# Projecting two bands at once and taking a group mean out earlier, in a four-layer convolution kernel

## The chip, the cores and the metric

The kernel runs as one launch on one core of a Trainium2 chip, in fp32 throughout. The metric is the device time of that launch in microseconds (us). The kernel before takes 4968.51 us, the median of three runs (4963.12 to 4970.23); the profiled execution that is read below spans 4964.9 us. The core has five engines with their own instruction queues: TensorE (PE in the profile, with its weight loads as PEld), VectorE (DVE), ScalarE (ACT), GpSimd (POOL) and SyncE (SP, which here only issues transfers).

## The reference

The input is 4 images of 384 channels and 64x64 positions. Four residual layers follow one another, each `x = x + layer(group_norm(x))` with 32 groups of 12 channels. Two of them matter here.

Layer 1 projects the normalised image to 384 hidden channels, filters every 8x8 patch of them in the frequency domain, runs a depthwise 3x3 convolution, multiplies one half of the channels (through a gelu) with the other half, and projects the 192 products back:

```
t = einsum('bchw,oc->bohw', x, w_in)
...                                     # patch filter, depthwise 3x3
x1, x2 = t[:, :hid // 2], t[:, hid // 2:]
g = gelu(x1) * x2
return einsum('bchw,oc->bohw', g, w_out)    # 192 -> 384 channels
```

Layer 3 is a depthwise 7x7 convolution whose 49 taps differ for every image and channel: `gamma * (x_w * w_mix * Nx) + beta`, where `x_w` comes from the mean and the maximum of each channel. Because `beta` is the same for all 49 taps, the kernel computes it as a 7x7 box sum, and the rest as a convolution with the fixed taps `w_mix` that is scaled per image and channel afterwards.

Layer 0 is a convolution with an attention over the 4096 positions; layer 2 consists of depthwise 3x3 and 5x5 convolutions and two channel projections (384 to 768 and back). Their code is not changed.

## The kernel before

The code is a Python builder that writes instructions in a program order; a list scheduler then orders them on each engine, by priority (the order of writing, unless a block is under `tc.high_priority()`), by what each waits for and by its estimate of when an engine is free. The engines then work through their queues in order. Tiles come from pools: a tag with `bufs=2` has two buffers in turn, and a new tile of the tag waits until the last reader of the tile before the previous one is done.

There are four stages, one after the other:

- `phase_a` (0 to 2533 us): layers 0 and 1. `side_by_side` (L529) takes the 64 steps of the attention of image b, and between them pieces of `others`: the norm of image b+1, its q, k and v, and layer 1 of image b-1. Each piece yields a cost in us of TensorE time, and `per_step` spreads the sum of these costs over the 64 steps. A step of the attention is four score products over 32 rows each (L715, under high priority), exponentials on ScalarE (L723) and four products over 128 rows (L752). Layer 1 of the last image runs alone, from 2290 us on.
- `phase_b` (to 3191 us): the depthwise convolutions of layer 2.
- `phase_ef` (to 4195 us): its channel projections, dense TensorE work.
- `phase_g` (to the end): the end of layer 2, the group norm and layer 3.

**Layer 1's projection back.** `layer1` (L797) works through 8 bands of 8 image rows. `band_taps` (L926) leaves the gated products of a band in two tiles: 128 channels in `acc[1]`, and 64 channels in rows 64 to 127 of `acc[2]`. `band_out` (L959), one piece per band, adds the projection to the band of x: for each of the three output blocks of 128 channels, a product over 128 rows (L965) and one over 64 rows (L966) accumulate in one PSUM tile, and VectorE adds it to x (L969). The PSUM tag "m" of this stage has two buffers. Each block yields 2.0 us.

**The beginning of phase_g.** `x2_of` (L1671) makes the input of layer 3 from what phase_ef left in memory, for one image and one block of 128 channels at a time, in four quarters of 1024 positions. ScalarE scales the second projection's result into PSUM (L1688, two of 512), VectorE adds it to x (L1691), ScalarE sums the squares (L1693) and VectorE takes the maximum (L1694). The finished tile of 2 MB goes to memory (L1696). The first block (j = 0) is brought into "strips", the layout of the convolution, by `to_strips` (L1699), one image behind: ScalarE subtracts the group's mean into another tile (L1710), TensorE transposes it in blocks of 128 (L1720), and ScalarE (L1727) and VectorE (L1725) copy the results to `z`.

**The rest of phase_g.** `conv7` (L1730) convolves 8 channels at a time: it loads their taps (`wmix`, L1735), expands them to matrices (L1744, every third on GpSimd) and multiplies (L1757). 48 such calls follow one another, 16 for each block of channels. In between, the first 16 take pieces of `x2_of` for the other two blocks; the other 32 take pieces of `boxes` (L1772), the box sums. `half_strips` (L1633) reads x2 of the next block from memory, scales and shifts it on ScalarE (L1649), transposes it and copies it to `z` (L1658, L1660). In `boxes`, x has its mean still in it, so constants of 6 or 7 means (`off`) are subtracted with every sum on VectorE (L1812 to L1823), and the padding is filled with means on ScalarE (L1793). L1837 adds the box sums to x, L1847 adds the convolution's result.

The transfers of x, of the taps and of the strips are all issued by SyncE, in one queue.

Of the kernel before, what the change touches and what calls it, by code (L numbers as in the profile page):

```python
# [27 lines left out]
N = H * W  # L28
# [132 lines left out]
def _layout(i):  # L161
# [38 lines left out]
    w_out_t[64:, 1] = w_out[P:]  # L200
# [26 lines left out]
class _Builder:  # L227
# [301 lines left out]
    def side_by_side(self, b, steps, others):  # L529

        per_step = ((176 if b else 0) + (42 if b + 1 < B else 0)) / 64
        ahead = 0.0
        for n, _ in enumerate(steps):
            while others is not None and ahead < n * per_step:
                piece = next(others, None)
                if piece is None:
                    others = None
                else:
                    ahead += piece
        for _ in others or ():  # L540
            pass
# [255 lines left out]
    def layer1(self, b):  # L797
# [9 lines left out]
        for n in range(-2, 4 * 11):  # L807
# [35 lines left out]
            if w == 0 and h > 2:  # L843
                k = h - 3
                yield from self.band_out(b, acc.pop(k), k, st)
# [80 lines left out]
    def band_taps(self, h, alone, acc):  # L926
# [9 lines left out]
        for j in range(NJ):  # L936
            acc.append(self.wk("acc", "acc", 5))
# [16 lines left out]
            if j == 2:  # L954
                nc.scalar.activation(acc[0][64:P], acc[2][0:64], AF.Gelu)
                nc.vector.tensor_mul(acc[2][64:P], acc[2][64:P], acc[0][64:P])
            yield

    def band_out(self, b, acc, h, st):  # L959

        nc = self.nc
        x = self.block("xa_out", self.xa[b], h, "xo", 2)
        for o in range(NJ):
            m = self.pa("out_m1") if b == B - 1 else self.pm("out_m")
            nc.tensor.matmul(m, lhsT=self.w_out[:, 0, o * P : (o + 1) * P], rhs=acc[1], start=True, stop=False)  # L965
            nc.tensor.matmul(  # L966
                m, lhsT=self.w_out[64:P, 1, o * P : (o + 1) * P], rhs=acc[2][64:P], start=False, stop=True
            )
            nc.vector.tensor_add(x[:, o], x[:, o], m)  # L969
            yield 2.0  # L970
        self.stats(st, x, h)
        nc.gpsimd.dma_start(self.x1[b][:, :, h * 512 : (h + 1) * 512], x)
# [487 lines left out]
    def phase_g(self):  # L1460
# [8 lines left out]
        with ExitStack() as ctx:  # L1469
# [26 lines left out]
            self.s_s, self.s_b = (cp.tile([P, NJ, B], F32, tag=k, name=k) for k in ("s_s", "s_b"))  # L1496
            self.a_pair = cp.tile([P, NJ, 2, 2, 2], F32, tag="a_pair", name="a_pair")

            self.gm = cp.tile([P, NJ, B], F32, tag="gm", name="gm")
            self.off = cp.tile([P, NJ, B, 3], F32, tag="off", name="off")  # L1500
# [7 lines left out]
            behind = iter(())  # L1508
            for b in range(B):
                for x in self.x2_of(0, b):  # L1510
                    next(behind, None)
                for _ in behind:
                    pass
                behind = self.to_strips(0, b, x)
            for _ in behind:
                pass
            self.pair_scales(1)
# [10 lines left out]
            for j in range(NJ):  # L1528
# [12 lines left out]
                if j == 0:  # L1541
# [3 lines left out]
                    self.pair_scales(2)  # L1545
# [5 lines left out]
    def group_means(self):  # L1551
# [4 lines left out]
        for i, k in enumerate((-6.0, -7.0, 2.0)):  # L1556
            nc.vector.tensor_scalar(self.off[:, :, :, i], self.gm, k, None, ALU.mult)
        nc.gpsimd.memset(self.s_s, 1.0)
        nc.vector.tensor_scalar(self.s_b, self.gm, -1.0, None, ALU.mult)
# [12 lines left out]
    def factors(self):  # L1572
# [3 lines left out]
        d, avg, mx = tile_of("g_d"), tile_of("g_avg"), tile_of("g_max")  # L1576
        nc.vector.tensor_sub(avg, self.mean2, self.gm)
# [9 lines left out]
        nc.vector.tensor_sub(mx, mx, self.gm)  # L1587
# [32 lines left out]
        nc.vector.tensor_copy(self.s_s[:, 2], self.a_s[:, 2])  # L1620
        nc.vector.scalar_tensor_tensor(self.s_b[:, 2], self.gm[:, 2], -1.0, self.a_s[:, 2], ALU.mult, ALU.mult)

    def pair_scales(self, j):

        for half in range(2):
            for u in range(2):
                for k, v in enumerate((self.s_s, self.s_b)):
                    self.nc.gpsimd.dma_start(
                        self.a_pair[64 * u : 64 * u + 64, j, k, half],
                        v[64 * half : 64 * half + 64, j, u::2],  # L1630
                    )

    def half_strips(self, j, half):  # L1633

        nc = self.nc
        for pair in range(2):
            for part in range(3):
# [10 lines left out]
                s, b = (self.a_pair[:, j, k, half, pair : pair + 1] for k in range(2))  # L1648
                nc.scalar.activation(y[:, inside], y[:, inside], AF.Identity, bias=b, scale=s)  # L1649
                for i, (k0, n) in enumerate(((0, 4), (4, 4), (8, 3))):  # L1650
# [6 lines left out]
                    if i == 1:  # L1657
                        nc.vector.tensor_copy(zv.rearrange("p c k b -> p k b c"), mv)  # L1658
                    else:
                        nc.scalar.copy(zv, mv.rearrange("p k b c -> p c k b"))  # L1660
# [10 lines left out]
    def x2_of(self, j, b):  # L1671

        nc = self.nc
# [3 lines left out]
        else:  # L1677
            x = self.gx_tile("x2")
            nc.sync.dma_start(x, self.wx[b][:, j])
        for q in range(4):  # L1680
# [4 lines left out]
            for v in range(2):  # L1685
                m = self.pm("x2_m")
                part = slice(q * 1024 + v * 512, q * 1024 + v * 512 + 512)
                nc.scalar.activation(  # L1688
                    m, h[:, v * 512 : v * 512 + 512], AF.Identity, bias=at(self.g0), scale=at(self.gh)
                )  # L1690
                nc.vector.tensor_add(x[:, part], x[:, part], m)  # L1691
# [3 lines left out]
            yield None  # L1695
        nc.gpsimd.dma_start(self.scratch["x2"][b][j], x)  # L1696
        yield x

    def to_strips(self, j, b, x):  # L1699

        nc = self.nc

        for part in range(3):
            y = self.gt_p.tile([P, 11 * P], F32, tag="y", name="ax2", bufs=2)
            lo, hi = (22 * part - 1) * W, (22 * part + 21) * W
            if part == 0:
                nc.gpsimd.memset(y[:, 0:W], 0.0)
            if part == 2:
                nc.gpsimd.memset(y[:, N - lo :], 0.0)
            nc.scalar.activation(  # L1710
                y[:, max(lo, 0) - lo : min(hi, N) - lo],
                x[:, max(lo, 0) : min(hi, N)],
                AF.Identity,
                bias=self.s_b[:, j, b : b + 1],
                scale=self.s_s[:, j, b : b + 1],
            )
            for i, (k0, n) in enumerate(((0, 4), (4, 4), (8, 3))):
                m = self.pm("strip_m")
                for k in range(n):
                    nc.tensor.transpose(m[:, k * P : (k + 1) * P], y[:, (k0 + k) * P : (k0 + k + 1) * P], self.ident)  # L1720
                mv = m.rearrange("p (k c) -> p k c", c=P)[:, 0:n, :]
                at = 1 + 11 * part + k0
                zv = self.z[:, :, at : at + n, b]
                if i == 1:
                    nc.vector.tensor_copy(zv.rearrange("p c k -> p k c"), mv)  # L1725
                else:
                    nc.scalar.copy(zv, mv.rearrange("p k c -> p c k"))  # L1727
            yield

    def conv7(self, j, c0):  # L1730
# [3 lines left out]
        wmix = self.gt_p.tile([P, 8 * 64], F32, tag="wmix", name="wmix")  # L1734
# [151 lines left out]
```

## Time and profile before

| stage | us | PE busy | DVE busy | ACT busy | POOL busy | GB/s |
|---|---|---|---|---|---|---|
| attention with layer 1 (640 to 2290 us) | 1650 | 1599.19 | 916.29 | 761.41 | 60.15 | 57 |
| layer 1 of the last image alone (2290 to 2533) | 243 | 231.16 | 181.61 | 103.06 | 10.19 | 92 |
| x2 and strips of the first block (4204 to 4290) | 86 | 36.52 | 58.40 | 80.84 | 8.74 | 304 |
| first 16 conv7 calls, x2 of two blocks (4290 to 4496) | 206 | 157.24 | 133.73 | 120.86 | 64.29 | 332 |
| next 16 calls with boxes (4496 to 4740) | 244 | 209.35 | 207.55 | 88.53 | 137.83 | 208 |
| last 16 calls with boxes (4740 to 4965) | 225 | 188.27 | 204.85 | 45.70 | 102.47 | 245 |

The table is the busy time of the engines in the stages that the change touches. Busy times of one engine are unions, so that two instructions that overlap count once; a PE busy all the time need not be at its peak, [...]. An fp32 product appears as two MATMUL passes, so 96 products are 192 instructions.

### The profile page before, as it was taken

What the parts mean: (1) busy time and instruction counts of PE and PEld (TensorE: products, weight loads), DVE (VectorE), ACT (ScalarE), POOL (GpSimd) and SP (SyncE); (2) the same over time, 40 slices, a digit from 0 to 9 for tenths busy, and PEclk for the clock granted to TensorE, in tenths of its full rate; (3) what the DMA queues carried; (4) which work ended last, traced back from release to release, by engine and by line L of the source; (5) the groups of instructions that cost most, each with busy time, mean ns of one, the idle gap of its engine ahead of it and who ended that gap; (6) DMA issues with size and microseconds to landing.
All of it is one profiled execution on the core that took longest, in us unless ns stands there. A gap on an engine that the chain in (4) does not pass through costs nothing.

```text
span 4964.9 us, 47732 instructions
## 1 busy us (share of the span) xinstructions
PE 4552.7 (92%) x17665; PEld 2564.5 (52%) x17665; DVE 2769.8 (56%) x4438; ACT 2136.4 (43%) x2873; POOL 777.5 (16%) x593
## 2 busy tenths in 40 slices
PE   5999999999999999998989999699999998677988
PEld 2343444434443344444557888444444443577888
DVE  5322465644666445555867778655531112667898
ACT  4444344454444444444435666411123333764321
POOL 1000000000000000000025555100000001125554
PEclk9999999999999999998989999799999999699999
DMA  5210211211111111112338999776664443896776
GB/s 169 73 47 30 85 54 55 72 56 39 64 64 51 55 45 58 58 57 78 120 122 276 291 292 292 250 278 256 256 245 157 153 152 132 316 343 203 239 255 227
DMA packets 346710, 752.64 MB, mean 152 GB/s; under 512 B 22779, under 2 KB 173158, under 8 KB 337510
## 3 DMA queue, kind: packets, MB, share of 16 engines
q1 hardware_dynamic: 280728, 475.46, 30.1%
q0 software_dynamic: 32640, 151.28, 7.9%
q10 hardware_dynamic: 33102, 122.77, 6.3%
q8 instruction: 143, 2.34, 0.2%
q14 instruction: 97, 0.79, 0.0%
HBM read 447.16 MB, written 302.25 MB: 151 GB/s over the span
## 4 chain that ended last, share of the span: by engine, by line
PE 45%; DVE 9%; DMA 4%; ACT 3%; issue 3%; POOL 1%; SPq 0%; ACTq 0%; DVEq 0%; POOLq 0%
PE h_s L1380 10%; PE h_m L1432 10%; PE conv_m L1156 9%; PE av L752 3%; PE t_m L871 2%; PE conv_m L1757 2%; DVE acc L948 2%; DMA wmix<-in_mix_t 1%; DMA g_h<-h 1%; PE out_m L966 1%; PE proj_m L785 1%; PE sc_s L715 1%; DVE toep L1744 1%; PE taps_m L941 1%; DVE toep L1137 1%
## 5 line engine op out<-in xcount | busy, mean ns | idle before, releaser
L752 PE MATMUL av<-probs,vt 128*128 128x512 f32 x2048 | 965.6, 607 | 0.0
L723 ACT ACTIVATE probs<-sc_s 128x1024 f32<-128x1024 f32 x512 | 500.9, 1021 | 789.8 <-PE av L752 783.7
L752 PEld LDWEIGHTS av<-probs,vt 128*128 128x128 f32 x2048 | 371.7, 192 | 468.1 <-issue 461.0
L1156 PE MATMUL conv_m<-toep,z 128*128 128x256 f32 x2304 | 519.4, 385 | 10.6 <-DVE toep L1137 5.1
L948 DVE SCALAR_TENSOR_TENSOR acc<-band,vecs,acc 128x512 f32<-128x512 f32 x708 | 496.9, 747 | 45.7 <-POOL band L909 39.9
L1432 PE MATMUL h_m<-f_h,cm_w_t 128*128 128x512 f32 x1152 | 496.7, 595 | 8.7 <-ACT f_h L1422 8.7
L1156 PEld LDWEIGHTS conv_m<-toep,z 128*128 128x128 f32 x2304 | 439.4, 193 | 71.0 <-DVE z L1089 4.9
L1757 PE MATMUL conv_m<-toep,z 128*128 128x128 f32 x3072 | 392.8, 286 | 42.1 <-DVE toep L1744 19.2
L1757 PEld LDWEIGHTS conv_m<-toep,z 128*128 128x128 f32 x3072 | 378.7, 202 | 44.4 <-POOL toep L1744 18.2
L1380 PE MATMUL h_s<-e_tok,cm_w_t 128*128 128x512 f32 x768 | 363.4, 596 | 5.5 <-DVE e_tok L1365 5.5
L1137 POOL TENSOR_TENSOR toep<-w,band 128x1536 f32<-128x1536 f32 x94 | 324.0, 3447 | 278.0 <-PE conv_m L1156 232.0
L1432 PEld LDWEIGHTS h_m<-f_h,cm_w_t 128*128 128x128 f32 x1152 | 220.0, 191 | 285.4 <-issue 273.3
L715 PE MATMUL sc_s<-q,k 32*128 32x512 f32 x2048 | 296.3, 647 | 21.9 <-ACT probs L723 21.4
L1440 DVE BATCH_NORM_STATS2 h_st<-f_h 128x6 f32<-128x512 f32 x96 | 66.4, 694 | 429.1 <-ACT f_h L1439 429.1
L871 PE MATMUL t_m<-w_in_t,xb 128*128 128x384 f32 x768 | 276.7, 495 | 3.4 <-DVE coef L888 2.1
L1387 ACT COPY e_h<-h_s 128x1024 f32<-128x1024 f32 x96 | 97.2, 1012 | 401.5 <-PE h_s L1380 401.5
L785 PE MATMUL proj_m<-xm,w_proj_t 128*128 128x512 f32 x576 | 265.2, 599 | 4.6 <-DVE xm L738 3.5
L792 DVE SCALAR_TENSOR_TENSOR x_res<-proj_m,bn_c,x_res 128x512 f32<-128x512 f32 x96 | 71.8, 748 | 319.0 <-PE proj_m L785 315.9
L1380 PEld LDWEIGHTS h_s<-e_tok,cm_w_t 128*128 128x128 f32 x768 | 147.0, 192 | 189.5 <-issue 183.2
L1389 DVE BATCH_NORM_STATS2 h_st<-e_h 128x6 f32<-128x512 f32 x192 | 123.4, 685 | 202.8 <-ACT e_h L1387 202.8
L871 PEld LDWEIGHTS t_m<-w_in_t,xb 128*128 128x128 f32 x768 | 142.9, 192 | 139.0 <-issue 59.3
L1380 PE MATMUL h_s<-z,cm_w_t 128*128 128x512 f32 x384 | 196.2, 593 | 0.0
(380 smaller groups left out, 6206.2 us busy)
## 6 DMA issues: line engine op xcount, KB each, us to landing
d<-d_o ACTq DMA_DIRECT2D x96, 512.0 KB
c_d<-d SPq DMA_DIRECT2D x96, 512.0 KB
hid<-e_h ACTq DMA_DIRECT2D x16, 3072.0 KB
f_h<-hid SPq DMA_DIRECT2D x16, 3072.0 KB
x_in<-in_x SPq DMA_DIRECT2D x96, 256.0 KB
x_res<-in_x SPq DMA_DIRECT2D x32, 768.0 KB
xa<-x_res POOLq DMA_DIRECT2D x32, 768.0 KB, 3.9
xa_in<-xa SPq DMA_DIRECT2D x32, 768.0 KB
```

What stands on the lines that cost most here:

```text
L715: nc.tensor.matmul(s[:, g], lhsT=k4[32 * g : 32 * g + 32, c], rhs=q[i][32 * g : 32 * g + 32], start=True, stop=True,)
L723: nc.scalar.activation(p[:, h * 1024 : (h + 1) * 1024], s[:, 2 * h : 2 * h + 2].rearrange("p a b -> p (a b)"), AF.Exp, scale=0.25,)
L752: nc.tensor.matmul(av, lhsT=vt[:, 4 * c + v, :], rhs=p[:, v * 512 : (v + 1) * 512], start=c == 0 and v == 0, stop=c == 7 and v == 3,)
L785: nc.tensor.matmul(m, lhsT=self.w_proj[:, j, o * P : (o + 1) * P], rhs=xm[:, j], start=j == 0, stop=j == NJ - 1,)
L871: nc.tensor.matmul(m[:, 0:C], lhsT=xb[:, j], rhs=self.w_in[:, j, :], start=j == 0, stop=j == NJ - 1,)
L948: nc.vector.scalar_tensor_tensor(out, src(j, k), w, done, ALU.mult, ALU.add)
L1137: eng.tensor_tensor(t, self.w53[:, at : at + 192].rearrange("p (m n) -> p m n", n=8).unsqueeze(2).to_broadcast([P, 24, 8, 8]), band.rearra ...
L1156: nc.tensor.matmul(m[:, c * 256 : (c + 1) * 256], lhsT=self.z_[:, at : at + P], rhs=t[:, 12 * c + 4 * i : 12 * c + 4 * i + 4].rearrange("p ...
L1380: nc.tensor.matmul(s[:, v, :], lhsT=w1[:, j, o * P : (o + 1) * P], rhs=t[j][:, v * 512 : (v + 1) * 512], start=j == 0, stop=j == NJ - 1,)
L1389: nc.vector.bn_stats(st[:, o, 8 * b + 2 * i + v, :], h[:, o, v * 512 : (v + 1) * 512])
L1432: nc.tensor.matmul(m, lhsT=w2[:, o, j * P : (j + 1) * P], rhs=h[:, o, v * 512 : (v + 1) * 512], start=o == 0, stop=o == 5,)
L1757: nc.tensor.matmul(m[:, ch * P : (ch + 1) * P], lhsT=self.z_[:, at : at + P], rhs=t[:, 8 * c + 2 * i : 8 * c + 2 * i + 2].rearrange("p m a ...
```

## The change

It has two parts that have nothing to do with each other.

**Two bands at once.** `bands_out` takes two bands after every second one. For each output block it holds two PSUM tiles: the two products over 128 rows are written first, then the two over 64 rows, which now lie in different halves of the array's rows, because the taps of even bands leave their 64 channels in rows 64 to 127 and those of odd bands in rows 0 to 63 (the weights are laid out twice). Products over different rows can run at the same time if they follow one another; to bring them together they are under high priority. A block yields 3.2 us for two bands, and `per_step` is fitted to that. The `acc` tag has six buffers in place of five.

**The mean out of x2.** The group's mean is subtracted from the coefficient `g0`, so that x2 is made without it: strips of the first two blocks need no scaling or shift and are transposed straight from x (`strips7`, quarter by quarter), the constants in `boxes` fall away, and padding is zero. The mean comes back where the result is finished, on ScalarE. In `x2_of` ScalarE works in place on 1024 positions, and VectorE adds from SBUF and no longer from PSUM. All copies of `half_strips` go to ScalarE. The taps of a call are loaded one call ahead.

```diff
-        per_step = ((176 if b else 0) + (42 if b + 1 < B else 0)) / 64
+        per_step = ((166 if b else 0) + (42 if b + 1 < B else 0)) / 64
...
-            if w == 0 and h > 2:
-                k = h - 3
-                yield from self.band_out(b, acc.pop(k), k, st)
+            if w == 0 and h > 3 and h % 2 == 0:
+                k = h - 4
+                yield from self.bands_out(b, (acc.pop(k), acc.pop(k + 1)), k, st)
...
-                nc.vector.tensor_mul(acc[2][64:P], acc[2][64:P], acc[0][64:P])
+                at = slice(0, 64) if h % 2 else slice(64, P)
+                nc.vector.tensor_mul(acc[2][at], acc[2][64:P], acc[0][64:P])
...
+            for m, acc in zip(ms, accs):
+                nc.tensor.matmul(m, lhsT=self.w_out[:, 0, to], rhs=acc[1], start=True, stop=False)
+            with tc.high_priority():
+                for i, (m, acc) in enumerate(zip(ms, accs)):
+                    at = slice(0, 64) if i else slice(64, P)
+                    nc.tensor.matmul(m, lhsT=self.w_out[at, 1, to], rhs=acc[2][at], start=False, stop=True)
+            for m, x in zip(ms, xs):
+                nc.vector.tensor_add(x[:, o], x[:, o], m)
+            yield 3.2
...
+        nc.vector.tensor_sub(self.g0, self.g0, self.gm)
...
-                s, b = (self.a_pair[:, j, k, half, pair : pair + 1] for k in range(2))
-                nc.scalar.activation(y[:, inside], y[:, inside], AF.Identity, bias=b, scale=s)
+                if j == NJ - 1:
+                    nc.scalar.activation(
+                        y[:, inside], y[:, inside], AF.Copy, scale=self.a_pair[:, half, pair : pair + 1]
+                    )
...
-                    if i == 1:
-                        nc.vector.tensor_copy(zv.rearrange("p c k b -> p k b c"), mv)
-                    else:
-                        nc.scalar.copy(zv, mv.rearrange("p k b c -> p c k b"))
+                    nc.scalar.copy(zv, mv.rearrange("p k b c -> p c k b"))
...
-            for v in range(2):
-                m = self.pm("x2_m")
-                part = slice(q * 1024 + v * 512, q * 1024 + v * 512 + 512)
-                nc.scalar.activation(
-                    m, h[:, v * 512 : v * 512 + 512], AF.Identity, bias=at(self.g0), scale=at(self.gh)
-                )
-                nc.vector.tensor_add(x[:, part], x[:, part], m)
+            nc.scalar.activation(h, h, AF.Identity, bias=at(self.g0), scale=at(self.gh))
+            nc.vector.tensor_add(x[:, sl], x[:, sl], h)
...
+            if j == 0:
+                self.strips7(b, x, q, edges)
...
-        wmix = self.gt_p.tile([P, 8 * 64], F32, tag="wmix", name="wmix")
-        nc.sync.dma_start(wmix, self.ins["mix_t"][j][:, c0 : c0 + 8].rearrange("p c t n -> p (c t n)"))
+        wmix = self.mix_ahead
+        self.mix_of(16 * j + c0 // 8 + 1)
...
-                nc.vector.tensor_scalar(hv[:, 0:2, 0], t[:, 0:2], off(6), None, ALU.add)
+                nc.scalar.copy(hv[:, 0:2, 0], t[:, 0:2])
...
-            nc.vector.scalar_tensor_tensor(
-                hv[:, 0:n, 1], pairs_of(x, r0 + 4, n)[:, :, 0], off(7), t[:, 0:n], ALU.add, ALU.add
-            )
+            nc.vector.tensor_add(hv[:, 0:n, 1], pairs_of(x, r0 + 4, n)[:, :, 0], t[:, 0:n])
             if part == 3:
-                nc.vector.tensor_scalar(hv[:, 6:8, 1], t[:, 6:8], off(6), None, ALU.add)
+                nc.scalar.copy(hv[:, 6:8, 1], t[:, 6:8])
...
+                if j == NJ - 1:
+                    nc.scalar.activation(xq, xq, AF.Identity, bias=self.gm[:, j, b : b + 1])
...
-                nc.vector.scalar_tensor_tensor(xp, d, self.a_s[:, j, b : b + 1], xp, ALU.mult, ALU.add)
+                nc.scalar.activation(
+                    d, d, AF.Identity, bias=self.gm[:, j, b : b + 1], scale=self.a_s[:, j, b : b + 1]
+                )
+                nc.vector.tensor_add(xp, xp, d)
```

## The prediction

> **What bounds the kernel now.** I first read the page's busy times: TensorE leads with 92%, but that is a mean over stages with different limits, so I asked for busy times by stage (columns: stretch, length, then busy us and instructions of PE, PEld, DVE, ACT and POOL, granted clock, share and GB/s of the transfers).
>
> ```profile
> 640.00:2290.00 1650.00, 1599.19 (x5265) 699.27 (x5263) 916.29 (x1514) 761.41 (x927) 60.15 (x117) 0.98 0.17 57
> 4204.00:4290.00 86.00, 36.52 (x136) 24.85 (x137) 58.40 (x68) 80.84 (x106) 8.74 (x18) 0.50 0.85 304
> 4290.00:4496.00 206.00, 157.24 (x1267) 154.50 (x1265) 133.73 (x153) 120.86 (x172) 64.29 (x39) 0.90 0.94 332
> 4496.00:4740.00 244.00, 209.35 (x1736) 201.97 (x1737) 207.55 (x252) 88.53 (x161) 137.83 (x99) 0.97 0.66 208
> 4740.00:4965.00 225.00, 188.27 (x1544) 183.21 (x1542) 204.85 (x207) 45.70 (x94) 102.47 (x63) 0.94 0.72 245
> ```
>
> Four limits show. With attention, TensorE (97%). While x2 of the first block is made, ScalarE (80.8 of 86 us). In the next 206 us the transfers: 94% at 332 GB/s; in 4345 to 4400 it is 351 GB/s at 97%. With boxes, VectorE (91% in the last stage) with TensorE (84%) close behind.
>
> Next the timeline of TensorE where layer 1 stands between attention steps (start, length, then the instruction; two passes make one fp32 product):
>
> ```profile
> 692.48 2.84 PE L752 MATMUL av<-probs,vt 128*128 128x512 f32 x6
> 695.15 1.02 PE L965 MATMUL out_m<-acc,w_out_t 128*128 128x512 f32 x2
> 696.11 1.12 PE L966 MATMUL out_m<-acc,w_out_t 64*128 64x512 f32 x2
> 697.16 1.13 PE L965 MATMUL out_m<-acc,w_out_t 128*128 128x512 f32 x2
> 698.21 1.14 PE L715 MATMUL sc_s<-q,k 32*128 32x512 f32 x8
> 699.28 1.12 PE L966 MATMUL out_m<-acc,w_out_t 64*128 64x512 f32 x2
> 700.34 3.70 PE L752 MATMUL av<-probs,vt 128*128 128x512 f32 x8
> ```
>
> From start to start, L752's eight passes take 3.44 us where no other width is near (708.39 to 711.83): 0.86 a product. L966 takes 1.05, and so does L965 between two changes of row width; with one change beside it L965 takes 0.96. A change of width thus costs 0.19 us, and a product over 64 rows as much as one over 128. Four score products over different 32 rows take 1.07, changes included: they run together. The score products beside L966 do not run with it, though the first two lie in other rows: 1.05 and 1.07 add up.
>
> Last the groups with their shortest, median and longest instruction:
>
> ```profile
> L1809 DVE TENSOR_TENSOR box<-box,box x48: 671/693/2874, 4496.4 to 4927.1; 128x512 f32<-128x512 f32 x48
> L1837 DVE SCALAR_TENSOR_TENSOR in_x<-box_m,b_s,in_x x96: 726/741/753, 4509.0 to 4951.7; 128x512 f32<-128x512 f32 x96
> L1812 DVE TENSOR_SCALAR box<-box,off x12: 268/404/2195, 4498.2 to 4899.9; 128x128 f32<-128x128 f32 x12
> L1658 DVE COPY z<-strip_m x24: 1060/1092/1118, 4383.2 to 4827.3; 128x512 f32<-128x512 f32 x24
> L1710 ACT ACTIVATE ax<-x,s_b,s_s x12: 1487/1493/1572, 4215.9 to 4282.8; 128x1344 f32<-128x1344 f32 x8, 128x1408 f32<-128x1408 f32 x4
> L1688 ACT ACTIVATE x_m<-g_h,g,gh x96: 756/771/797, 4208.4 to 4478.4; 128x512 f32<-128x512 f32 x96
> ```
>
> VectorE instructions with SBUF operands alone (L1809, L1812) sometimes last some 2 us longer; L1837 and L1658, which read PSUM, never do. [...]
>
> [...]
>
> **The change part by part.**
>
> *Two bands at once.* The halves gain only if they follow one another, so what matters is where the scheduler puts them. I compared the order of TensorE's instructions in the two built programs; before's is the order of its trace. With high priority, the first 64-row product goes ahead as soon as its own 128-row product is written, in front of the other band's. Of 96 products over 64 rows, 86 stand alone and ten in five pairs; by their tiles one pair has opposite halves. The saving of up to 48 x 0.86 = 41 us shrinks to 0.9. And the second half, at the same priority as the scores, lands inside them: in 23 of 256 groups one score product comes before it and three after. Those four no longer run together: 23 x 0.86 = 19.8 us. Changes of width rise by 17: 3.2 us. Sum 19.8 + 3.2 - 0.9 = 22 us, on an engine with 3% idle time there. VectorE's adds stay 96, in pairs; the taps queued behind them have slack (56% busy). At the end of the last image two bands in place of one follow the last taps. In the order two more products over 128 rows and two over 64 come after them: 4 x 0.86 less what fits into the wait for the taps (3.3 us before), 3 us for bounds of 0 and 6. Together +25; bounds +10 (part of the score split hides in waits) and +32.
>
> *x2 and strips of the first block (86 us).* ScalarE loses 12 x 1.5 = 18 us (L1710); 32 x 0.77 becomes 16 of 1024 positions at 1.235 (L1077, the same operation in place): -5; the copies to z go from 24 x 0.975 to 16 x 1.08 (L1117) and 4 x 0.3: -5. So 81 becomes 53. VectorE: [...] 4 more copies at 1.09, +4: 60. VectorE would be the limit, some 20 us earlier. The transposes now wait for each quarter's add; behind them on TensorE stand only other transposes. But the first two stages move 86 x 304 + 206 x 332 = 94.5 MB, which the change leaves as it is. At 332 GB/s this takes 285 us, at 351 it takes 269, against 292 now. The gain is 7 to 23; I take -12, at 337. Taps ahead by one call change the order in SyncE's queue, not the bytes: their waits (65 us in the chain) are the transfers' limit seen from TensorE; I cost them at nothing.
>
> *Boxes (469 us).* VectorE loses 18 copies (of L1658's 24, six lie in the earlier stage) x 1.09 = 20, 12 x 0.65 (L1812) and 12 x 0.45 (L1823) = 13. 164 additions become simpler by about 0.06 (L948's 747 against L953's 683 for 512), the short ones by less: 7. Sum 40 of 412 us. ScalarE gains about 57 us on 134 (32 x 0.72 for the mean, 32 x 1.23 for the convolution's scale, 18 x 0.58 and 24 x 0.3 for copies, less 6 x 1.5 and the fills) and stays below half. It is in order, though: queued behind an instruction that waits for VectorE are the copies L1831, for which TensorE waits (36 us idle on ht in these stages), and new instructions of that kind are added. With VectorE alone as limit the gain is 40, with TensorE at 398 of 469 us less. I take half, -20, and -2 for GpSimd's eight small transfers of the third block's scales that become four (0.64 us each, on the chain at 4509 us). Bounds -5 and -42.
>
> The stages between have the same order in both programs: nothing. Sum: +25 - 12 - 22 = -9, or 4959 us.
>
> **The rivals.** *Layer 1's loss stays, phase_g gives little:* transfers stay at 332 GB/s (-7), and TensorE and ScalarE's in-order waits take over in the boxes (-6): +25 - 13 = +12, 4980 us, slower. For it: 94% transfer share, TensorE at 84 to 86%. Against: VectorE's 91%. *phase_g gives all:* -20 and -42 with +25: -37, 4931. For it: VectorE's share in the last stage and ScalarE's 94% in the first. Against: the bytes. *The halves run together after all,* and the scores too: -41 and -34: 4893. Against it: L966 and the scores in other rows take 1.05 and 1.07 us one after the other in this trace.
>
> **How the numbers follow.** The likeliest case 0.48, layer 1's loss 0.24, phase_g in full 0.22, halves together 0.06. Within 0.2% means 4958.6 to 4978.4; the likeliest case lies at its edge and gives 0.22 faster, 0.20 same, 0.06 slower. With the rivals, faster is 0.22 + 0.22 + 0.06 = 0.50; same 0.20 + 0.06 (the nearer part of the slower rival) = 0.26; slower 0.06 + 0.18 = 0.24. The range, 4930 to 4985, takes in both middle rivals and leaves out the halves and the ends of the bounds (+32 with little gain).
>
> **What would show it.** The attention stage should be 15 to 30 us longer with TensorE as full as before, and its timeline show two score passes, the 64-row product, six score passes. If the halves stood together, two of them would take 1.05 us. The stage of the first strips should end 12 to 20 us earlier with ScalarE near 53 us of work, and the next stage stay above 0.94 in transfers. In the boxes VectorE's busy time should fall by some 40 us, and TensorE's share rise. The forecast is wrong if layer 1 costs nothing, if the x2 stages shrink below 269 us, or if the boxes shrink by more than VectorE's 40.

## The result, and the profile after

The changed kernel takes 4997.43 us (median; 4994.91 to 5002.69) against 4966.11 us of the kernel before beside it: a ratio of 1.0064, 95% interval 1.0046 to 1.0081. It is slower by some 31 us, where 4959 with a range to 4985 was predicted.

The two profiled executions (4964.9 and 4994.0 us) show where. The stages are cut at events that both have: the first convolution of phase_b, the first product of phase_ef, the last `h_m` product, the first `conv7` product.

| stage | before | after | difference | predicted |
|---|---|---|---|---|
| phase_a (to the first product of phase_b) | 2556.6 | 2579.6 | +23.0 | +25 |
| phase_b | 634.7 | 643.8 | +9.1 | 0 |
| phase_ef | 1002.4 | 1003.4 | +1.0 | 0 |
| x2 and strips of the first block, to the first `conv7` product | 95.4 | 83.5 | -11.9 | -12, with the x2 of the other blocks |
| `conv7`, the other x2, boxes | 675.8 | 683.7 | +7.9 | -22 |

The copy or addition that ends each of the 48 `conv7` calls divides the last row: 165 us before and 161 after from the 1st to the 16th, 264 and 274 to the 32nd, 229 and 233 to the 48th. The cut at the last x2 instruction that the prediction used puts 1920 `conv7` passes of TensorE into the boxes before and 2023 after, so its 469 us and the 504 below don't hold the same work of the convolution; the calls do.

The view of busy times by stage, of the kernel after, with the columns of the prediction (attention, the two x2 stages, the boxes in two parts):

```profile
640.00:2290.00 1650.00, 1605.53 (x5219) 695.98 (x5218) 916.11 (x1502) 757.00 (x918) 60.26 (x116) 0.99 0.16 56
4226.00:4310.00 84.00, 36.06 (x148) 28.65 (x146) 62.38 (x89) 59.48 (x76) 8.00 (x20) 0.53 0.81 296
4310.00:4490.00 180.00, 137.49 (x1118) 134.33 (x1119) 125.73 (x109) 99.09 (x130) 55.97 (x33) 0.91 0.99 360
4490.00:4740.00 250.00, 212.28 (x1675) 207.49 (x1674) 162.48 (x205) 112.17 (x203) 135.28 (x107) 0.90 0.65 206
4740.00:4994.00 254.00, 214.52 (x1756) 208.74 (x1755) 208.79 (x219) 85.46 (x141) 120.20 (x81) 0.95 0.72 239
```

Attention is as full as before. The second x2 stage runs at 360 GB/s and a share of 0.99: the transfers do give what was hoped for, up from 332 and 0.94 before. In the boxes VectorE is busy 371 us in place of 412, the 40 us that were predicted; between the ends of the 16th and the 48th call it is 379 in place of 423, in part because x2 ends earlier. They bought no time, and TensorE's share of the boxes, which should have risen, stays at 85% (427 of 504 us, 398 of 469 before).

TensorE's timeline of the kernel after, with the split that the order of the program had promised (two passes make a product):

```profile
744.30 1.13 PE L970 MATMUL out_m<-acc,w_out_t 128*128 128x512 f32 x2
745.35 1.12 PE L715 MATMUL sc_s<-q,k 32*128 32x512 f32 x2
746.40 1.12 PE L974 MATMUL out_m<-acc,w_out_t 64*128 64x512 f32 x2
747.46 1.13 PE L715 MATMUL sc_s<-q,k 32*128 32x512 f32 x6
748.52 3.70 PE L752 MATMUL av<-probs,vt 128*128 128x512 f32 x8
```

From start to start one score product takes 1.05 us, the product over 64 rows 1.06, the other three score products 1.06. Unsplit, the four take 1.07, as the timeline of before showed.

The instructions of the boxes that answer to those shown of before (shortest, median and longest, in ns); L1822 and L1832 are new:

```profile
L1796 DVE TENSOR_TENSOR box<-box,box x48: 673/693/3230, 4504.9 to 4951.8; 128x512 f32<-128x512 f32 x48
L1820 DVE SCALAR_TENSOR_TENSOR in_x<-box_m,b_s,in_x x96: 736/745/752, 4516.1 to 4982.1; 128x512 f32<-128x512 f32 x96
L1822 ACT ACTIVATE in_x<-in_x,gm x32: 704/722/727, 4516.9 to 4669.0; 128x512 f32<-128x512 f32 x32
L1832 ACT ACTIVATE in_raw<-in_raw,gm,a_s x32: 1238/1242/1298, 4674.8 to 4977.2; 128x1024 f32<-128x1024 f32 x32
```

The durations are those predicted. What changed is who waits. The waits of the kernel before in the boxes (who waited for whom, us in all, times, longest):

```profile
PE box_m L1835 <- ACT ht L1831: 35.7, 22, 5.3
DVE in_x L1837 <- PE box_m L1835: 16.4, 11, 4.3
```

and of the kernel after:

```profile
ACT in_raw L1832 <- DMA in_raw<-raw: 65.2, 19, 7.0
DVE in_x L1820 <- PE box_m L1818: 49.4, 30, 4.7
PE box_m L1818 <- ACT ht L1814: 46.9, 22, 5.2
DVE box L1796 <- POOL box L1795: 27.8, 21, 5.7
```

ScalarE waits 65 us for loads that hardly anybody had waited for (VectorE 1.2 us before). TensorE waits longer for ScalarE's copies of `ht`, and VectorE waits 33 us more for TensorE's box sums and 13 us more for GpSimd's (14.7 before): about as much as it no longer works.

### The profile page after: what moved, and what is told of

Its sections match the earlier page's. It is cut to its first block, busy times and chain, and to the rows that moved or that the text cites. A ratio compares the mean times of both kernels' runs of the same rounds, so it can differ in the third digit from the quotient of the medians.

```text
span 4994.0 us, 47605 instructions
## 1 busy us (share of the span) xinstructions
PE 4591.5 (92%) x17665; PEld 2587.0 (52%) x17665; DVE 2723.4 (55%) x4341; ACT 2149.2 (43%) x2881; POOL 781.9 (16%) x608
## 5 line engine op out<-in xcount | busy, mean ns | idle before, releaser
L715 PE MATMUL sc_s<-q,k 32*128 32x512 f32 x2048 | 323.6, 650 | 21.5 <-ACT probs L723 21.3
L715 PEld LDWEIGHTS sc_s<-q,k 32*128 32x128 f32 x2048 | 88.4, 186 | 215.3 <-ACT probs L723 137.5
```

The costliest lines, as they stand in the source:

```text
L715: nc.tensor.matmul(s[:, g], lhsT=k4[32 * g : 32 * g + 32, c], rhs=q[i][32 * g : 32 * g + 32], start=True, stop=True,)
```

## The experiments

Theories when they began: (1) the instructions that the change put on ScalarE hold up, in its fixed order, the copies of `ht`; rivals were (2) the taps' early place in SyncE's queue, (3) a hand-over in which no one engine sets the pace, and TensorE alone. For phase_b's 9 us there was no theory yet. Ratios are to the kernel before, with 95% intervals; 0.001 is 5 us. Stage times are of one profile each; how far one is to be trusted is seen from five kernels whose `conv7` stage is that of before in all but place: 675.8 to 679.3 us. Line numbers in the text are those of the kernel after, in a view those of its own kernel.

| kernel | phase_a | phase_b | to `conv7` | `conv7` to end | ratio |
|---|---|---|---|---|---|
| before | 2556.6 | 634.7 | 95.4 | 675.8 | |
| after | 2579.6 | 643.8 | 83.5 | 683.7 | 1.0064 (1.0046 to 1.0081) |
| a_only | 2591.8 | 635.8 | 94.6 | 679.3 | 1.0060 (1.0042 to 1.0078) |
| a_low | 2543.3 | 638.1 | 95.1 | 679.0 | 0.9981 (0.9972 to 0.9989) |
| a_first_low | 2535.4 | 636.3 | 95.2 | 677.9 | 0.9948 (0.9932 to 0.9964) |
| b_pad | 2555.4 | 639.3 | 95.2 | 676.4 | 1.0015 (1.0008 to 1.0023) |
| g_only | 2558.2 | 642.3 | 83.9 | 682.0 | 1.0004 (0.9995 to 1.0012) |
| g_raw_dve | 2562.1 | 643.8 | 84.4 | 678.1 | 0.9991 (0.9981 to 1.0002) |
| g_taps_late | 2553.6 | 639.9 | 84.0 | 686.2 | 1.0004 (0.9995 to 1.0013) |
| g_pe3 | 2551.4 | 644.2 | 84.2 | 658.5 | 0.9932 (0.9912 to 0.9952) |
| g_align | 2556.6 | 635.2 | 84.0 | 676.1 | 0.9982 (0.9974 to 0.9989) |
| h_no_add | 2563.8 | 634.1 | 83.0 | 679.3 | 0.9970 (0.9957 to 0.9983) |
| h_pipe | 2557.9 | 638.3 | 84.6 | 685.1 | 0.9985 (0.9977 to 0.9992) |
| h_early | 2552.0 | 637.5 | 84.3 | 687.7 | 0.9997 (0.9987 to 1.0007) |
| h_z | 2554.0 | 642.2 | 83.9 | 671.8 | 0.9973 (0.9961 to 0.9986) |
| h_no_gm | 2556.6 | 638.0 | 83.3 | 674.6 | 0.9974 (0.9967 to 0.9980) |
| h_raw | 2557.3 | 638.4 | 83.8 | 661.8 | 0.9963 (0.9949 to 0.9977) |
| h_old_act | 2554.3 | 637.9 | 83.6 | 660.1 | 0.9947 (0.9929 to 0.9965) |
| best1 | 2531.2 | 640.1 | 82.5 | 679.9 | 0.9936 (0.9920 to 0.9953) |
| best2 | 2530.9 | 638.6 | 83.1 | 659.3 | 0.9907 (0.9891 to 0.9924) |

### Each part alone

**a_only** is the kernel before with `bands_out` and what belongs to it; `edge` moves to the pool `g_t` to make room for the sixth `acc` buffer.

> The kernel before with layer 1's two bands alone (one small buffer of the boxes stands in another pool, to make room). Theory: the split score products and the width changes are all of this part, 23 us before the first convolution of the next stage and nothing after it: 4989 us. Rival: the 9 us that the next stage is longer in the changed kernel follow from this part too: 4998 us. If the part costs nothing alone, 4966.

The ratio 1.0060 is 30 us; the expected 4989 is 1.0046, inside the interval. The profile's 35 us in phase_a may hold some of another kind: from 2290 us to the last `out_m` its granted clock is 0.93, in the profile after 0.94, before 0.97. phase_b has 635.8 us, so the 9 us of the changed kernel there don't follow from this part.

**g_only** is the changed kernel with layer 1 as before.

> The changed kernel with layer 1 as before. Theory: counted by the calls of the last convolution, the first strips give 12 us and its first 16 calls 5, and the boxes take 14 more: about 4963 us, 32 less than the changed kernel, boxes stage slow as there. Rival: the boxes lose only because of what happens in layer 1 or in the stage after it (a different run, a different clock): then 4966 - 12 - 5 - 22 = 4927.

1.0004: 2 us slower, not the 4963 that the theory gave. Its profile shows what the theory had left out: phase_b, whose instructions are those of before in the same order, has 642.3 us. The two parts together, 30 and 2 us, make up the 31.

### Layer 1: where the scheduler puts the halves

**a_first_low** drops the high priority and turns the products round:

```diff
-            for m, acc in zip(ms, accs):
-                nc.tensor.matmul(m, lhsT=self.w_out[:, 0, to], rhs=acc[1], start=True, stop=False)
-            with tc.high_priority():
-                for i, (m, acc) in enumerate(zip(ms, accs)):
-                    at = slice(0, 64) if i else slice(64, P)
-                    nc.tensor.matmul(m, lhsT=self.w_out[at, 1, to], rhs=acc[2][at], start=False, stop=True)
+            for i, (m, acc) in enumerate(zip(ms, accs)):
+                at = slice(0, 64) if i else slice(64, P)
+                nc.tensor.matmul(m, lhsT=self.w_out[at, 1, to], rhs=acc[2][at], start=True, stop=False)
+            for m, acc in zip(ms, accs):
+                nc.tensor.matmul(m, lhsT=self.w_out[:, 0, to], rhs=acc[1], start=False, stop=True)
```

> Layer 1's two bands alone, but without the high priority, and with the products over 64 rows put first: they begin the two sums, and the products over 128 rows end them. In this program's order 37 pairs of opposite halves stand next to each other (5 pairs in the changed kernel), no group of four score products is split (23 there), and the row width changes 620 times (675 before, 692 changed). Theory (only the order keeps the halves apart, and adjacent ones run together): 37 x 0.86 + 55 x 0.19 = 42 us less, 3 more at the end of the last image: about 4930 us, and the timeline shows two 64-row products in some 1.05 us. Rival (halves do not run together): only the 10 us of width changes less 3, 4962.

**a_low** drops the high priority alone.

> The kernel before with layer 1's two bands alone, without the high priority, the products over 128 rows first as in the changed kernel. In this order 16 pairs of opposite halves are adjacent, no group of four score products is split, and the row width changes 624 times. Theory (only adjacency, splits and changes count): 16 x 0.86 + 51 x 0.19 - 3 = 20 us less than before, 4951. Rival (the high priority is not the cause of the loss, the two bands are): slower than before, 4985 or more.

Timeline of TensorE in a_first_low; the second line holds both halves, four passes:

```profile
1329.64 2.31 PE L752 MATMUL av<-probs,vt 128*128 128x512 f32 x5
1331.88 1.13 PE L971 MATMUL out_m<-acc,w_out_t 64*128 64x512 f32 x4
1332.94 1.12 PE L973 MATMUL out_m<-acc,w_out_t 128*128 128x512 f32 x2
```

Two products over 64 rows take 1.06 us together, as long as one before. Apart, each of them takes that time for itself (1.06 us from 746.40 in the timeline after): the gain needs them as neighbours in TensorE's queue. So the idea of the change holds, and its priority undoes it: with the priority alone gone, the loss of 30 us becomes a gain of 9, with the order turned as well 26. The count promised more, 39 us for a_first_low and 20 for a_low; as built, 13 of a_low's 16 pairs are of opposite halves (and one of the changed kernel's five), which makes its count 18. In a_first_low TensorE's busy time from 640 us to the last `out_m` falls by 30 us (1829.90 to 1799.55), while its idle time rises from 62 to 71: part of the missing gain goes into waits.

### phase_b: an address

**b_pad** adds one tile to the kernel before; **g_align** adds this tile to g_only, and one of 288 bytes in phase_g:

```diff
+        pad = self.sm([P, 16], "pad", 1)
+        nc.gpsimd.memset(pad, 0.0)
```

> The kernel before with one more tile of 64 bytes a partition, filled once; every buffer that is allocated behind it, those that transfers fill in the second layer's stage among them, moves by 64 bytes. Nothing else differs. Theory (the 8 us that this stage is longer in all three kernels with the changed last part come from this shift: there its buffers lie 64 bytes off a multiple of 128, and its transfers take 69% of the engines' time in place of 64.6): this stage 642 us instead of 635, transfers' share 0.91 instead of 0.86, in all about 4976. Rival (the 8 us come from elsewhere): stage 635, 4969.

> As g_only, with two unused tiles that move the buffers of the second layer's stage and of the last part back to multiples of 128 bytes. Theory: second layer's stage back to 635 us (from 642), share of the transfers 0.86; if the loads of the last part suffer too, its transfers' share at the boxes falls and they get up to 5 us shorter: 4958 to 4965. Rival (address plays no part): as g_only, 4972.

The transfer queues in phase_b (packets, MB, the share of 16 engines' time that their packets took), first of the kernel before, then of b_pad, then of g_align:

```profile
q1 hardware_dynamic: 119119, 121.32, 64.4%
q10 hardware_dynamic: 14292, 52.77, 21.1%
```

```profile
q1 hardware_dynamic: 119165, 121.45, 68.4%
q10 hardware_dynamic: 14292, 52.77, 21.3%
```

```profile
q1 hardware_dynamic: 119087, 121.22, 64.6%
q10 hardware_dynamic: 14292, 52.77, 21.1%
```

The same bytes cost q1, SyncE's queue, which mostly loads, 7% more time when the buffers that they fill lie 64 bytes off (68.4% of 639.3 us against 64.4% of 634.7); q10, ScalarE's queue, which mostly stores, 2%. The split is clean over all kernels of the table: 63.7 to 64.6% in the fourteen whose load buffers for x, the weights and the convolutions' results in phase_b start at multiples of 256 bytes, 68.2 to 69.1% in the six where they start 64 bytes beside one (b_pad, after, and all g_ kernels but g_align). phase_b's own time is less clean: 634.1 to 642.2 us in the fourteen, 637.5 in the mean, and 639.3 to 644.2 in the six, 642.2 in the mean. So some 5 of the 9 us are the address's; the rest is no more than the fourteen differ among themselves. b_pad is slower by 1.0015 (8 us), g_align faster than g_only by some 11 us, of which 7 in phase_b. Whether phase_g gains from it too (676.1 against 682.0 us) isn't settled, with kernels of one last part 3.5 us apart. In the changed kernel the shift comes from small tiles that were removed or moved to another pool: 64 bytes were left over. It is the written side of the transfers, in SBUF, that moves; why this costs them time isn't shown.

### The boxes: which engine sets the pace

**g_pe3** lets `conv7` add three products in place of four (`for i in range(3)`); **h_no_add** is g_align without L1835, VectorE's addition of the convolution's values.

> As g_only, but the last convolution adds up three of its four products per channel and place, so a part of its kernel is left out of the output. TensorE loses 768 products of 0.129 us, 99 us, in the last part; nothing else changes. Theory (TensorE's in-order stream with its waits is what sets the pace of the boxes, not VectorE): 60 to 90 us less, 4880 to 4910. Rival (VectorE or ScalarE sets the pace): under 20 us less, 4952 or more.

> As g_align, but VectorE's 32 additions of the convolution's values (1.22 us each, 39 us) are left out, and so is this sum in the output of blocks 0 and 1; ScalarE still scales the values. If VectorE's work still sets the pace of the boxes: 25 to 39 us less there, 4925 to 4940. If the hand-over does, or ScalarE's waits for the loads: under 10 us less, 4955 or more.

TensorE gives back 24 us (profile) to 36 us (ratio, to g_only) of 99, all between calls 16 and 32, none behind call 32 (229 us in both). VectorE gives back 6 of 39 by the ratio, 0 by the calls (501 us from the 16th to the 48th, 499 in g_align). Neither sets the pace alone after the change.

**g_taps_late** loads the taps at the call again; **h_pipe** transposes and copies both halves of a part before it multiplies them.

> As g_only, but the taps of each call of the convolution are loaded when the call begins, as before the change, and not one call ahead. Theory 2 (SyncE's queue stands at the early load until the taps' buffer is free, 118 us in the boxes, and the loads of strips and of the convolution's values stand behind it): 10 to 20 us below g_only, and ScalarE's wait for the loaded values well below 65 us. Rival (ScalarE's order alone): boxes as in g_only; the stage of x2 perhaps 5 us longer.

> As g_align, same work, but in each part both halves are transposed and copied first, then both are multiplied, with the break for the convolution between. Theory 3 (hand-over): TensorE's waits for ScalarE's copies of ht, 40 to 47 us in the boxes, fall to under 25, and the time by 10 to 25 us: 4940 to 4954. If VectorE, the loads or ScalarE's total set the pace: no gain, 4960 to 4970.

Neither edit mends it: g_taps_late is as slow as g_only (1.0004 each, its first 16 calls take 168 us in place of 162, the next four 77 in place of 83), and h_pipe as g_align (266 us in place of 273 to call 32, 239 in place of 226 behind it). So the early taps are not the cause, and this order of the hand-over doesn't help; others were not tried.

### The boxes: what ScalarE was given

**g_raw_dve** is g_only with one edit: VectorE scales and adds the convolution's values again.

```diff
-                nc.scalar.activation(
-                    d, d, AF.Identity, bias=self.gm[:, j, b : b + 1], scale=self.a_s[:, j, b : b + 1]
-                )
-                nc.vector.tensor_add(xp, xp, d)
+                nc.vector.scalar_tensor_tensor(xp, d, self.a_s[:, j, b : b + 1], xp, ALU.mult, ALU.add)
```

> As g_only, but VectorE scales and adds the convolution's values of blocks 0 and 1 in one instruction as before; ScalarE's pass over them is gone, and with it the mean of those two blocks, which is left out of the output. Theory (ScalarE waits in order for the loads of these values, 65 us, and the copies that TensorE needs stand behind): 10 to 25 us below g_only, 4940 to 4953, and ScalarE's wait for transfers gone. Rival (the loss lies in the other new ScalarE instructions or in the taps' place in the queue): within 5 us of g_only.

It gave 4 to 6 us, less than the theory and at the edge of its rival. So the next kernel took everything back. **h_old_act** is g_align with this edit, L1822 left out, and the copies of L1799, L1806 and the middle one of L1654 on VectorE.

> As g_align, but every instruction that the change put on ScalarE in the boxes is taken off it: the middle copies to z and the short copies at the edges go back to VectorE, which also scales and adds the convolution's values in one instruction again, and the additions of the mean (both kinds) are left out of the output. VectorE keeps its simpler additions. Theory 1 (ScalarE's new in-order work took the gain): from the first call of the last convolution to the end 655 to 665 us (676 in g_align and in the kernel before). Theory 3 (no single engine sets the pace; TensorE, ScalarE and VectorE hand each half of a part to one another in fixed order, and VectorE's freed time is spent waiting for box_m): 672 to 680, as before.

660.1 us, and 17 us by the ratio below g_align: theory 1. From the 16th to the 48th call it takes 484 us, where g_align takes 499 and the kernel before 493. Its waits in the boxes:

```profile
PE box_m L1817 <- ACT ht L1813: 29.7, 15, 4.9
DVE in_x L1819 <- PE box_m L1817: 21.1, 15, 5.3
```

In g_align they are 43.0 and 46.2 us; here both are about where they were before the change (35.7 and 16.4). VectorE is busy 408 us in these calls, 15 less than before, and part of this shorter work now shows as time. The next kernels divide it: **h_z** takes back the copies alone, **h_no_gm** leaves out L1822 (the pass that adds block 2's mean) alone, **h_raw** takes back the passes over loaded values (L1832) and leaves out L1822.

> As g_align, but only the middle copies to z (18 of them beside the boxes, 1.08 us each) and the short copies at the edges go back from ScalarE to VectorE; ScalarE keeps the scaling of the convolution's values and the mean of block 2. If these copies are what holds up ScalarE's copies of ht: from the first call of the last convolution to the end 660 us, as with everything taken back (676 in g_align), 4947 in all. If it is the other two kinds: 676, 4964. If both have a share: some 668, 4956.

> As g_align, but ScalarE's 32 passes over block 2 (0.72 us each, 23 us) are left out, and with them the mean of block 2 in the output. h_raw without these and without the passes over the loaded values has 662 us from the first call to the end, g_align 676. If block 2's passes take their part: 666 to 670, shorter by 6 or more in calls 16 to 32. If all of it is the loaded values: 675 or more.

> As g_align, but only the convolution's values go back to VectorE (one instruction scales and adds) and the mean of all three blocks is left out of the output, so ScalarE has no pass over x or over loaded values in the boxes; the copies to z and at the edges stay with it. If its waits for the loads (54 to 65 us) and for VectorE's in_x (11 to 17 us) hold up the copies of ht: 660 us from the first call to the end, 4947. If the copies do: 676, 4964. If both have a share: some 668, 4956.

Against g_align, the copies give 4 us by profile and ratio (0.9973 against 0.9982, intervals overlap), block 2's pass 1.5 and 4 (0.9974), it and the passes over loaded values together 14 and 9 (661.8 us; 0.9963). The copies and the passes so add up to about the 16 to 17 of h_old_act. The loaded values look like the largest share, though alone (g_raw_dve) they gave 4 to 6 us; the single shares are hardly above the noise. **h_early** asks whether it is their wait alone: the load is issued at the start of its part, the work stays.

> As g_align, with the same work on every engine, but each load of the convolution's values is issued at the start of its part, two breaks earlier. If ScalarE's wait for these loads is what costs (54 us in calls 32 to 48 of g_align): the wait under 20 us and 662 to 668 us from the first call to the end (676), 4950 to 4957 in all. If the pass itself, with VectorE's addition waiting behind it, costs: 674 or more, although the wait is shorter. If the earlier load only waits for a free buffer in SyncE's queue: the wait stays, 676 or more.

Its waits in the boxes, and those of SyncE's queue:

```profile
ACT in_raw L1829 <- DMA in_raw<-raw: 52.6, 16, 7.0
```

```profile
SPq L1781 <- DVE in_x L1832: 91.6, 21, 9.5
```

The third case: the load now waits for one of the three buffers, which VectorE's addition sets free. The wait in ScalarE stays at 53 us, and the kernel is some 7 us slower than g_align (0.9997 against 0.9982). So the wait alone could not be taken away, and the share of the wait and of the pass itself stays open.

### Both parts, mended

**best1** joins a_first_low and g_align. **best2** also takes the copies and the scaling back to VectorE and keeps the mean: ScalarE adds it to the finished sum.

```diff
+                nc.vector.scalar_tensor_tensor(xp, d, self.a_s[:, j, b : b + 1], xp, ALU.mult, ALU.add)
+                nc.scalar.activation(xp, xp, AF.Identity, bias=self.gm[:, j, b : b + 1])
```

> The changed last part with its buffers on multiples of 128 bytes (g_align) and layer 1's two bands with the 64-row products first and no high priority (a_first_low) together. The two parts lie in stages that do not touch, so the ratios should multiply: 0.9982 x 0.9948 = 0.993, about 4936. If the parts interact, [...] 0.996 or more, 4950.

> As best1 (halves adjacent, buffers on multiples of 128 bytes), but in the boxes the copies to z and at the edges are VectorE's again, and VectorE scales and adds the convolution's values; the mean is complete: ScalarE adds it to the finished sum, as the last thing done to each piece, so that nothing else waits for this pass. If only what stands ahead of the copies of ht costs time: most of the 17 us that h_old_act has over g_align, 4922 to 4930. If any in-order pass of ScalarE behind VectorE holds the copies up: 4936 to 4942, as best1.

best1 has 0.9936, about the product of its parts, 0.993; best2 0.9907, 46 us faster than the kernel before. Its waits in the boxes, L1839 the pass with the mean:

```profile
ACT in_x L1839 <- DVE in_x L1838: 73.4, 29, 5.7
DVE in_x L1826 <- PE box_m L1824: 22.4, 21, 3.0
```

ScalarE waits longer here than for the loads in the kernel after, 73 us, and no time is lost against h_old_act, which leaves the mean out (659.3 and 660.1 us). So it isn't the amount of ScalarE's work or waiting that costs, but its place. The likely reason why this place is free, argued and not shown: it waits for VectorE, whose next sums the next copies of `ht` need in any case. In the kernel after it waits nearly as long for transfers, with VectorE's addition behind it.

## Why the prediction was wrong

- *Two bands at once, +25:* right (+23; a_only, alone, 30 by the ratio). The split scores, the single halves and the width changes are in the timeline as counted. The granted clock is no rival for the sum: it is 0.98 from 640 us to the last `out_m` in both profiles, a little higher after the change during attention (0.99 for 0.98) and lower behind it (0.94 for 0.97). That halves would run together as neighbours was given a chance of 0.06, and was rightly not expected of this order; a_first_low shows it in another.
- *x2 and strips, -12:* about right at equal work of the convolution: -12 to the first `conv7` product and -4 in the first 16 calls. ScalarE's 53 us are 59, VectorE's 60 are 62 (they counted 2 us less for 16 additions of 1024, the author's estimate; these take 1.22 us each, where two of 512 took 1.37), and the two stages together move 340 GB/s on the mean (84 us at 296, 180 at 360) where 337 was taken. By the prediction's own cut they take 264 us in place of 292, below the 269 that it named as a sign of being wrong. Two of its assumptions failed there: the second stage went above the 351 GB/s (4345 to 4400 us of before) taken as the most, with 360, and the bytes didn't stay, 90 MB in place of 94.5, because x2 ends earlier and part of the convolution moved into the boxes. That the sum came near is in part luck.
- *Stages between, nothing:* wrong by 9 us. The step compared the order of instructions, which is the same, and not the addresses. b_pad and g_align show that 64 bytes are worth some 5 of them in this stage, on the mean of the kernels; the rest lies within the spread of single profiles.
- *Boxes, -22:* the failed step, +8 in the `conv7` stage, +14 from its 16th call to the 48th. VectorE's 40 us were sized rightly. Half of them was put down as gain because ScalarE "stays below half". It does (198 of 504 us, 64 more than before where 57 were summed; the terms written there make 71, less some 8 for the fills), but it stands ahead of TensorE: what it was given holds up the copies of `ht` (TensorE waits 46.9 us for them, 35.7 before), and costs as much as VectorE's relief brings. g_align, with the addresses put right, takes 499 us from the 16th to the 48th call, 493 before; without ScalarE's additions it is 484 (h_old_act). With them, another 39 us off VectorE give next to nothing (h_no_add). That VectorE's 91% was the limit before is made likely by the 484, and not shown: the early x2 and taps are in it too. The bounds, -5 and -42, didn't let the sign turn, though the text named the waits in ScalarE's order; the slower rival had this mechanism with -6 in place of a loss.
- *The sum:* -9 was +31. Of these 40 us some 34 are the boxes' step and 9 phase_b; the x2 stages gave 4 more than predicted. Up to 6 us of the boxes' part may be the addresses in phase_g (682.0 us in g_only, 676.1 in g_align), which isn't settled.

## What to carry to other kernels

Work moved from a full engine to a half-idle one isn't free because that engine has time: ask what stands behind it in that engine's queue. Here it was free as the last touch of a result, behind the engine that was relieved (best2 659.3 us, and 660.1 without it in h_old_act), and dear between a load and that engine (g_align 676.1 us, and 661.8 without it and block 2's pass in h_raw). High priority doesn't keep two instructions together (86 of 96 products over 64 rows stood alone); look in the program's order for what lands between them. When tiles are added, dropped or moved between pools, compare the start addresses of all later buffers that transfers fill: a stage that nobody touched lost 0.7% here (642.2 for 637.5 us, the means).

## What was not expected of the hardware

Loads into buffers 64 bytes off a multiple of 256 took 7% more of the transfer engines' time for the same bytes (68.4% of 639.3 us for 64.4% of 634.7), and the whole kernel 0.15% more (b_pad). Offsets other than 64 bytes above or below were not tried, so a multiple of 128 may do as well. The granted clock differs between executions of nearly the same TensorE work (0.957 to 0.963 over the kernels' profiles). Where layer 1 ends, from 2290 us to the last `out_m`, it is 0.97 before, 0.94 after and 0.93 in a_only. An estimate of what that is worth there is some 10 us (258.7 us of TensorE time of a_only times 1 - 0.93/0.97); it takes TensorE's time to go with the clock, which no run here isolates.
